# A four-layer transformer kernel on one core: layer 0 with x^T stored by tile, its last projections inside the block FFN, its indices outside the pool, and loads issued in the order of use

## The chip, the core and the metric

The kernel runs on one core of a Trainium2 chip. The core has a matrix engine (TensorE, here PE, with its weight loads as PEld), three other compute engines (VectorE is DVE, ScalarE is ACT, GpSimd is POOL), and an engine that mostly issues DMAs (SyncE, SP), which move data between HBM and the on-chip memory. The metric is the time of one launch on the device in microseconds (us), lower is better; a verdict compares medians of several runs.

## The reference, cut to what matters

Two batches of 1024 tokens with 1024 features pass through four layers, in fp32. Every layer is post-norm: `x = layernorm(x + attn(x))`, then `x = layernorm(x + ffn(x))`. The change touches layer 0 and the entry of layer 1. Batch 0 goes through all four layers before batch 1 begins.

```python
# layer 0, attention: 8 heads of 16 features
qk = (x @ Wqk_w.T + Wqk_b).reshape(b, n, 8, 16, 2)
v = (x @ Wv_w.T + Wv_b).reshape(b, n, 8, 16)
scores = einsum('bhqd,bhkd->bhqk', q, k)
attn = softmax(scores) / 128 ** 0.5
out = einsum('bhsl,bhlv->bhsv', attn, v) -> (b, n, 128)
x = layernorm(x + out @ Wo_w.T + Wo_b)
# layer 0, FFN: the features permuted, in 16 blocks of 64 -> 256 -> 64
t = x[:, perm].reshape(b * n, 16, 64)
t = gelu(einsum('bhd,hdm->bhm', t, up))
t = einsum('bhm,hmd->bhd', t, down).reshape(b * n, 1024)[:, unperm]
x = layernorm(x + t)
# layer 1, attention, its first step: a convolution of width 3 along the tokens, to 3 x 256 features
q, k, v = split(conv(x, conv_w) + conv_b, 3)
```

Layers 2 (a state space scan) and 3 (attention and a mixture with low-rank experts) are left as they are.

## The kernel before, in words

**Where things lie.** `x` holds one batch on chip, tokens on the 128 partitions, in 8 token tiles of 1024 features. `xT` is its transpose, features on partitions, in 8 tiles `k` of 128 features by 1024 tokens, with a column of margin at each end. Weights come into a pool `w` of 8 buffers of 512 KB, in turn. `ps` are the 8 banks of the matmul accumulator (PSUM), also taken in turn. Small vectors live in pools that open and close with the layer's stages; a tile that takes the place of another one in such a pool waits for its last reader.

**Order.** In layer 0 and at the entry of layer 1 the order of the work is written out by hand (`manual_schedule`): each engine issues its instructions in program order, and SP issues the DMAs in program order too, so that a DMA that waits for something holds up all DMAs behind it on SP. Gathers and scatters by index are issued by POOL.

**Layer 0, `l0(b)`.** First all eight tiles of `x` are loaded for batch 0 (`load_x`, before `l0` is called; for batch 1 the tiles are loaded by the end of the last layer, as they come free), and tiles 0 to 3 are turned into `xT` (`to_xT`, L130). Then `l0` issues its loads in this order: the three parts of `wqkv`, `wo`, the row of the bias `l0_bo`, two `up` and two `down`, and in its own pool `bqkv` and `idx`, the permutation. A *half* `th` is 512 tokens, four token tiles.

1. `qkv(s, th, scalar)` (L257) makes q, k or v for a half; for q and k, eight small DMAs spread the heads over the partitions.
2. `maxima(th)` computes the scores once for the maximum of each row (L292), with the remaining `qkv` steps between.
3. `attend(th, extra)` computes for each of 16 steps `n` (two groups of four heads, eight tiles of keys) the scores again (L327), their exponentials (ACT, L335) and the outputs (PE, L345); `done(g)` (copy `oT` L352, transposes L355) normalizes a group into `ao`. `extra[n]` is other work, placed behind step `n`'s outputs. In `attend(1)` it is the projection of the first half.
4. `project(tt)` transposes one tile of `ao` (L388), copies it on DVE to `aoT` (L390), multiplies it by `wo` in two matmuls of 512 columns (L393), adds them to `x` (`add_x`, L152) and takes the norm's statistics. `line(th, first, n)` spreads over the steps of the stage that runs beside: `first` of four tiles, then the roots and the scaling of all four, then four times `to_xT`. The list `n` gives the step of each.
5. `store(th)` writes a half of `xT` to HBM as `xd`, in eight DMAs of 256 KB, one for each feature tile, with runs of 2 KB (L399). `gather(th, n)` reads it back, by `idx`, with one indirect DMA for each tile `t` of 128 permuted features (L406).
6. `blocks(th, extra)` is the block FFN of a half. For each `j` of 8: `ups(j)` (four matmuls, L424), `gelus(j)` on ACT (L432), `downs(j)` (four matmuls, L442), a copy `o` (DVE, L454) and an indirect scatter into `yd` (POOL, L455). `ups(j+1)` stands ahead of `downs(j)`; `extra[j]` comes behind `downs(j)`.
7. `back(th)` loads `yd` (L473), and `add_y(tt, ys)` transposes it and adds it to `x`. For half 0 this runs beside `blocks(1)`, for half 1 at the entry of layer 1.

Between `attend(1)` and `blocks(0)` nothing runs beside: `done(1)`, `project(4)` and `project(5)` stand by themselves; `project(6)`, `project(7)`, roots, scaling and `to_xT` of the second half lie in `blocks(0)` at j = 0, 0, 1, 2, 2, 3, 3; `store(1)` is at j = 3, `gather(1)` at 5, 6 and 7.

**Entry of layer 1, `l1_attn(b)`.** Four small loads (`l1_convb` first, L85) go to a pool that takes the place of layer 0's. The convolution of a half is computed in a form with four products of half the length: `conv(th, co)` for each of six output tiles `co`. Its `load()` fetches the weights g0, g1, g2 (`w<-l_conv`, L80); for batch 0 and the first half, DVE computes t = g0 + g2 + g1 and t - 2 g1 from them (L599, L600, L601) and SP stores both to `cvd` (L603); everywhere else they are loaded from there. `sums0(j)` computes on DVE, in two pieces of four feature tiles each, a sum or difference of neighbouring tokens (L579) into a quarter of `qh` or `kh`, which `call(j, k)`, the convolution's matmuls (L612), read. `cb2` (L563) is twice the bias. The order is: c0's load and arithmetic, `sums0(0)`, `sums0(1)`, c1's load and arithmetic, the loads of `yd` half 1 (L652), then the matmuls, the rest of the sums, and the `add_y` of tiles 4 to 7 between them.

Of the kernel before, what the change touches and what calls it, by code (L numbers as in the profile page):

```python
# [17 lines left out]
P = 128  # L18
# [3 lines left out]
NT = S // P  # L22
# [5 lines left out]
class Net:  # L28
# [7 lines left out]
    def __init__(self, ctx, tc, ins, out):  # L36
        self.tc, self.nc, self.i, self.out = tc, tc.nc, ins, out
        nc = self.nc
        self.const = ctx.enter_context(tc.tile_pool(name="const", bufs=1))
        self.wp = ctx.enter_context(tc.tile_pool(name="wp", bufs=WB))  # L40
        self.bp = ctx.enter_context(tc.tile_pool(name="bp", bufs=2))
        self.sp = ctx.enter_context(tc.tile_pool(name="sp", bufs=3))
        self.pp = ctx.enter_context(tc.tile_pool(name="pp", bufs=8, space=PSUM))
        self.dp = ctx.enter_context(tc.tile_pool(name="dp", bufs=1, space=DRAM))
        self.count = 0
        self.evacs = 0

# [12 lines left out]
        nc.gpsimd.memset(self.one, 1.0)  # L60

        self.sel = c.tile([P, 4, 32], F, name="sel")
        nc.sync.dma_start(self.sel, self.i["l2_sel"])


    def nm(self, s):
# [146 lines left out]

    def l0(self, b):
        nc, i = self.nc, self.i
        wqkv = [self.w(i["l0_wqkv"][j]) for j in range(3)]
        wo = self.w(i["l0_wo"])
        row = self.row("l0_bo")
        up = [self.w(i["l0_up"][j]) for j in range(2)]
        down = [self.w(i["l0_down"][j]) for j in range(2)]  # L220
        xd, yd = [[self.dp.tile([D, HALF], F, name=self.nm(n)) for _ in range(2)] for n in ("xd", "yd")]
        with self.tc.tile_pool(name=self.nm("l0a"), bufs=1) as lp, self.tc.tile_pool(name=self.nm("l0b"), bufs=2) as tp:
            bias = self.param(lp, "l0_bqkv", [P, 3])
            idx = self.param(lp, "l0_perm", [P, KD], I)

            def piece(name):
                return lp.tile([P, HALF], F, tag="t", bufs=24, name=self.nm(name))
# [86 lines left out]
                        nc.vector.tensor_tensor(qT[g][th], qT[g][th], p, ALU.add)  # L314
                    yield

            def attend(th, extra):
# [55 lines left out]
                for n in range(N):  # L373
                    if n + 1 < N:
                        exps(n + 1)
                    if n + 2 < N:
                        scores(n + 2)
                    outputs(n)
                    if n == NT:
                        done(0)  # L380
                    for f in extra.get(n, []):
                        f()
                done(1)


            def project(tt):
                p = self.ps()
                nc.tensor.transpose(p[:, :P], ao[:, tt, :], self.ident)  # L388
                aoT = tp.tile([P, P], F, tag="aoT", name=self.nm("aoT"))
                nc.vector.tensor_copy(aoT, p[:, :P])  # L390
                for nh in range(2):
                    p = self.ps()
                    nc.tensor.matmul(p, aoT, wo[:, nh * HALF : (nh + 1) * HALF], start=True, stop=True)  # L393
                    self.add_x(tt, nh, p)
                self.ln_stats(tt)

            def store(th):
                for k in range(KD):
                    nc.sync.dma_start(xd[th][k * P : (k + 1) * P, :], self.xcols(k, th * HALF, HALF))  # L399

            ts = {0: [], 1: []}

# [6 lines left out]
                    )  # L409
                    ts[th].append(t)  # L410

            def blocks(th, extra):

                gls = {}

# [42 lines left out]
                    )  # L458

                ups(0)  # L460
                gelus(0)
                for j in range(KD):
                    if j + 1 < KD:
                        ups(j + 1)
                        gelus(j + 1)
                    downs(j)
                    for f in extra.get(j, []):
                        f()
# [21 lines left out]
            def at(extra, n, f):  # L490
                extra.setdefault(n, []).append(f)

            got = {}
            with self.tc.manual_schedule():
# [17 lines left out]
                m = maxima(1)  # L512
                attend(0, {n: [lambda: next(m)] for n in range(16)})
                e = line(0, project, (0, 1, 3, 4, 5, 6, 7, 8, 9))
                at(e, 9, lambda: store(0))
                at(e, 9, lambda: gather(0))
                attend(1, e)
                project(4)
                project(5)
                e = line(1, project, (-1, -1, 0, 0, 1, 2, 2, 3, 3))  # L520
                del e[-1]
                at(e, 3, lambda: store(1))
                for n in (5, 6):
                    at(e, n, lambda: gather(1, 2))
                at(e, 7, lambda: gather(1, 4))
                blocks(0, e)
                ys = back(0)
                e = line(0, lambda tt: self.add_y(tt, ys), (2, 3, 3, 4, 5, 6, 6, 7, 7))
                blocks(1, e)
# [6 lines left out]
    def l1_attn(self, b, yd, op):  # L536
        nc, i = self.nc, self.i
        row = self.row("l1_projb")
        with self.tc.tile_pool(name=self.nm("l1a"), bufs=1) as lp, self.tc.tile_pool(name=self.nm("l1s"), bufs=2) as spool:
# [20 lines left out]
            kh = lp.tile([P, 8, HALF], F, name=self.nm("kh"))  # L560
            u0 = lp.tile([P, HALF], F, name=self.nm("u0"))
            cb2 = lp.tile([P, 6], F, name=self.nm("cb2"))
            nc.vector.tensor_scalar(cb2, cb, 2.0, None, ALU.mult)  # L563
            if b == 0:
                self.cvd = self.dp.tile([6, 2, P, D], F, name=self.nm("cvd"))

# [24 lines left out]
            def conv(th, co):  # L591
# [3 lines left out]
                def load():  # L595
                    g = [self.w(i["l1_conv"][co, 0])]
                    if b == 0 and th == 0:
                        g1, g2, t = self.w(i["l1_conv"][co, 1]), self.w(i["l1_conv"][co, 2]), self.w()
                        nc.vector.tensor_tensor(t, g[0], g2, ALU.add)  # L599
                        nc.vector.tensor_tensor(t, t, g1, ALU.add)  # L600
                        nc.vector.scalar_tensor_tensor(g1, g1, -2.0, t, ALU.mult, ALU.add)  # L601
                        for n, f in enumerate((t, g1)):
                            nc.sync.dma_start(self.cvd[co, n], f)  # L603
                        w["w"] = [t, g1, g[0], g2]
                    else:
                        es = [self.w(self.cvd[co, n]) for n in range(2)]
                        w["w"] = es + g + [self.w(i["l1_conv"][co, 2])]
# [26 lines left out]
                return load, [lambda j=j, k=k: call(j, k) for j in range(4) for k in range(KD)], last  # L634

            def sums0(j):
                for g in range(2):
                    ks = slice(4 * g, 4 * g + 4)
                    sums(nc.vector, 0, ks, [(j, (qh, kh)[j // 2][:, ks, 256 * (j % 2) : 256 * (j % 2) + 256])])


# [2 lines left out]
            c0, c1 = conv(0, 0), conv(0, 1)  # L644
            with self.tc.manual_schedule():
                c0[0]()
                sums0(0)
                sums0(1)
                c1[0]()
                ys = [t for q in range(4) for t in (vh[:, q, :HALF], vh[:, q, HALF:])]  # L650
                for k, t in enumerate(ys):
# [1359 lines left out]
```

## Time and profile before

| what | value |
|---|---|
| runs of the kernel | 5103.77, 5097.98, 5096.71 us; median 5097.98 |
| the profiled execution | 5091.48 us, span in the trace 5089.7 us |
| mean granted clock of PE | 0.966 |
| busy: PE, PEld, DVE, ACT, POOL | 91%, 44%, 62%, 38%, 41% |
| the queues of SP's DMAs | 683.88 MB, 46.6% of 16 engines |

The span is from the first instruction to the last; the execution's own time is 1.8 us longer. The runs lie within 0.14% of each other. Times below "at" some point are microseconds from the start of the span. Batch 0's layer 0 runs from the start to about 326 us, batch 1's from 2545 to about 2858.

### The profile page before, as it was taken

How to read it: one execution, taken by the hardware profiler on the slowest of the kernel's cores; microseconds unless marked ns; L12 is line 12 of the kernel's file. 1: busy time of each engine (PE TensorE's matmuls, PEld its weight loads, DVE VectorE, ACT ScalarE, POOL GpSimd, SP SyncE). 2: the span in 40 equal slices, each digit the busy share in tenths (PEclk: the TensorE clock that was granted, in tenths of full speed). 3: DMA queues.
4: the chain of work that ended last, by engine and by line, in shares of the span. 5: the costliest groups of instructions: out<-in, count | busy, mean ns of one | idle time of the engine just before them, and what ended most of it. 6: DMA issues, size and time to landing. Idle time of an engine off the chain costs nothing. (4 is left out here: it accounts for less than half of the span.)

```text
span 5089.7 us, 49066 instructions
## 1 busy us (share of the span) xinstructions
PE 4656.9 (91%) x16584; PEld 2227.5 (44%) x16584; DVE 3152.2 (62%) x4322; ACT 1941.6 (38%) x3973; POOL 2094.1 (41%) x1259
## 2 busy tenths in 40 slices
PE   8989989988888889999999899899888988899999
PEld 3347745433333333454433576554333333334544
DVE  5453256389999996215365422652999999953153
ACT  2431232377665662001024212324776756510010
POOL 2013121089888994100020320201887989831010
PEclk9999999999999999999999999999999999999999
DMA  2144312488878997201211532113888889961100
GB/s 89 36 160 144 98 49 75 135 220 232 236 207 239 254 253 221 73 33 46 73 44 40 180 116 85 55 52 117 217 224 227 218 240 249 248 210 60 55 20 33
DMA packets 254862, 707.98 MB, mean 139 GB/s; under 512 B 37008, under 2 KB 54544, under 8 KB 254612
## 3 DMA queue, kind: packets, MB, share of 16 engines
q1 hardware_dynamic: 248340, 683.88, 46.6%
q0 software_dynamic: 6272, 20.98, 1.2%
q8 instruction: 132, 2.16, 0.2%
q14 instruction: 118, 0.97, 0.1%
HBM read 599.60 MB, written 86.25 MB: 135 GB/s over the span
## 5 line engine op out<-in xcount | busy, mean ns | idle before, releaser
L1299 POOL TENSOR_TENSOR h<-h,br 128x1024 f32<-128x1024 f32 x512 | 1205.7, 2372 | 105.8 <-DMA h<-dxd 71.1
L1306 PE MATMUL ps<-hl,rep 128*128 128x512 f32 x1024 | 733.5, 720 | 176.2 <-DVE h L1313 143.5
L1308 ACT ACTIVATE ps<-ps,l_Alog 128x512 f32<-128x512 f32 x1024 | 662.5, 662 | 554.4 <-PE ps L1306 551.8
L1313 DVE TENSOR_TENSOR_SCAN h<-ps,hst,h 128x512 f32<-128x512 f32 x512 | 633.4, 1282 | 19.9 <-ACT ps L1308 13.4
L1324 DVE TENSOR_TENSOR h<-h,ps 128x1024 f32<-128x1024 f32 x512 | 616.8, 1205 | 2.1 <-ACT hst L1321 2.0
L1313 DVE TENSOR_TENSOR_SCAN h<-ps,h 128x512 f32<-128x512 f32 x512 | 599.3, 1211 | 16.2 <-ACT ps L1308 16.1
L1421 PE MATMUL ps<-xT,w 128*128 128x512 f32 x1024 | 546.0, 620 | 10.1 <-DVE h L1313 8.9
L1306 PEld LDWEIGHTS ps<-hl,rep 128*128 128x128 f32 x1024 | 200.5, 197 | 600.3 <-DVE h L1313 436.0
L1626 POOL TENSOR_TENSOR x<-x,row 128x1024 f32<-128x1024 f32 x48 | 112.3, 2351 | 795.7 <-PE ps L130 795.7
L152 DVE TENSOR_TENSOR x<-x,ps 128x512 f32<-128x512 f32 x192 | 129.1, 684 | 435.1 <-PE ps L1803 143.9
L104 PE MATMUL ps<-xT,w 128*128 128x512 f32 x768 | 335.9, 592 | 0.0
L1335 PE MATMUL ps<-h,sel 128*32 128x512 f32 x2048 | 297.1, 630 | 5.6 <-DVE h L1324 5.6
L1459 PE MATMUL ps<-w,w 128*128 128x512 f32 x512 | 279.2, 629 | 21.3 <-DMA w<-yd 14.3
L177 ACT ACTIVATE rs<-mv 128x1 f32<-128x1 f32 (+2 forms) x88 | 17.9, 203 | 705.4 <-DVE mv L171 705.0
L1421 PEld LDWEIGHTS ps<-xT,w 128*128 128x128 f32 x1024 | 190.7, 195 | 204.4 <-issue 165.8
L104 PE MATMUL ps<-w,xT 128*128 128x512 f32 (+1 forms) x768 | 278.3, 522 | 0.0
L1366 PE MATMUL ps<-xT,w 128*128 128x512 f32 x512 | 271.6, 630 | 6.2 <-DVE h L1313 6.2
L1124 DVE SCALAR_TENSOR_TENSOR ps<-xp,l_convw,ps 128x512 f32<-128x512 f32 x192 | 145.1, 756 | 200.8 <-ACT ps L1119 196.2
L767 POOL TENSOR_TENSOR s<-s,l1r 128x512 f32<-128x512 f32 x64 | 66.5, 1040 | 487.8 <-DVE l1r L766 481.9
L1800 PE MATMUL ps<-w,xT 128*128 128x512 f32 x512 | 225.7, 594 | 0.0
L1244 POOL TENSOR_TENSOR e<-e,one 128x512 f32<-128x512 f32 x64 | 81.5, 1274 | 349.5 <-ACT xp L1116 220.3
L104 PEld LDWEIGHTS ps<-xT,w 128*128 128x128 f32 x768 | 145.0, 189 | 183.0 <-issue 178.1
(289 smaller groups left out, 7452.1 us busy)
## 6 DMA issues: line engine op xcount, KB each, us to landing
h<-dxd SPq DMA_DIRECT2D x512, 512.0 KB, 7.9
w<-l_in SPq DMA_DIRECT2D x128, 512.0 KB, 6.4
w<-l_out SPq DMA_DIRECT2D x96, 512.0 KB, 6.9
w<-l_conv SPq DMA_DIRECT2D x54, 512.0 KB, 3.8
w<-cvd SPq DMA_DIRECT2D x36, 512.0 KB, 3.3
w<-l_fw SPq DMA_DIRECT2D x32, 512.0 KB, 4.5
xcd<-xo SPq DMA_DIRECT2D x64, 256.0 KB, 3.9
xi<-xcd SPq DMA_DIRECT2D x64, 256.0 KB, 8.7
```

Of the source, the lines that this page charges most:

```text
L104: self.nc.tensor.matmul(out, lhsT, rhs, start=j == 0, stop=j == n - 1)
L1124: nc.vector.scalar_tensor_tensor(p, xp[:, k : k + HALF], cw[:, c, k : k + 1], p, ALU.mult, ALU.add)
L1299: nc.gpsimd.tensor_tensor(hs[k], hs[k], norms[of(k)[0]][1].unsqueeze(1).to_broadcast([P, 2, HALF]), ALU.mult)
L1306: nc.tensor.matmul(dA[k, m], rep[:, 4 * m + q, :], hl[u, c][:, jj, :], start=True, stop=True)
L1308: nc.scalar.activation(dA[k, m], dA[k, m], AF.Exp, scale=A[:, g : g + 1])
L1313: nc.vector.tensor_tensor_scan(hs[k][:, m, :], dA.pop((k, m)), hs[k][:, m, :], hst[:, g : g + 1] if u else 0.0, ALU.mult, ALU.add)
L1324: nc.vector.tensor_tensor(hs[k], hs[k], norms[of(k)[0]][3].unsqueeze(1).to_broadcast([P, 2, HALF]), ALU.mult)
L1335: nc.tensor.matmul(py[u, c][32 * j : 32 * j + 32, :], self.sel[:, q, :], hs[k - 1 + j // 2][:, j % 2, :], start=False, stop=q == 3,)
L1366: nc.tensor.matmul(p, w["w"][:, k * P : (k + 1) * P], self.xcols(k, u0, HALF), start=k == 0, stop=k == KD - 1)
L1421: nc.tensor.matmul(p, w["w"][:, k * P : (k + 1) * P], self.xcols(k, u * HALF, HALF), start=k == 0, stop=k == KD - 1)
L1459: nc.tensor.matmul(p, y[:, cc, t * P : (t + 1) * P], wt[:, cc * HALF : (cc + 1) * HALF], start=c2 == 0 and cc == 0, stop=last,)
L1800: nc.tensor.matmul(p, self.xcols(k, tt * P, P), wt[k][:, ns], start=k == 0, stop=False)
```

## The change

- *Loads.* Only tiles 0 to 3 of `x` are loaded before `l0`. In `l0`, part 1 and then part 0 of `wqkv` are loaded first, for batch 0 then `bqkv`, `idx`, `sel` (a constant of layer 2 that was the first load of the program) and tiles 4 to 7 of `x`, and then part 2 of `wqkv`, `wo` and the rest.
- *Indices outside the pool.* `bqkv` and `idx` are constants, loaded once, and no longer tiles of layer 0's pool in each batch.
- *Stores by tile.* `store(tt)` writes one token tile of `xT`, all features, in one DMA of 512 KB with 1024 runs of 512 bytes. The four of half 0 stand at n = 6 to 9 of `attend(1)`, each behind the `to_xT` of its tile; the four of half 1 at j = 3, 3, 4, 4 of `blocks(0)`.
- *Projections.* `turn_o` (the transpose and the copy `aoT`) is split from `project`. In `attend(1)` it stands ahead of the outputs of the same step, the rest behind them. The last `done(1)` runs inside `blocks(0)`, behind `ups(0)`; projections 4 to 7 lie at j = 0, 0, 1, 1 of `blocks(0)`, with their transposes ahead of `downs(j)`; roots and scaling at j = 2, `to_xT` at 3, 3, 4, 4.
- *Layer 1.* For batch 0, `sums0(0)` stands between L600 and L601 of `conv(0, 0)`; in both batches it comes in three pieces (feature tiles 0 and 1, 2 and 3, 4 to 7). `cb2` comes behind `sums0(1)`.

In the changed kernel's lines: `turn_o` is L401 and L403, the projection's matmuls L410, `store` L415, the gather L425, ups, gelus, downs, `o` and the scatter L443, L451, L461, L473, L474, `back` L496, the sums L601, the weight arithmetic L621, L622 and L625, the stores to `cvd` L627, the convolution's matmuls L636, `cb2` L674.

```diff
@@ __init__
-        nc.sync.dma_start(self.sel, self.i["l2_sel"])
+        self.idx = c.tile([P, KD], I, name="idx")
+        self.bqkv = c.tile([P, 3], F, name="bqkv")
@@ l0
-        wqkv = [self.w(i["l0_wqkv"][j]) for j in range(3)]
+        wqkv = {j: self.w(i["l0_wqkv"][j]) for j in (1, 0)}
+        if b == 0:
+            for t, name in ((self.bqkv, "l0_bqkv"), (self.idx, "l0_perm"), (self.sel, "l2_sel")):
+                nc.sync.dma_start(t, i[name])
+            for tt in range(4, NT):
+                self.load_x(0, tt)
+        wqkv[2] = self.w(i["l0_wqkv"][2])
...
-            bias = self.param(lp, "l0_bqkv", [P, 3])
-            idx = self.param(lp, "l0_perm", [P, KD], I)
+            bias = self.bqkv
+            idx = self.idx
@@ attend(th, extra, ahead={})
                     if n + 2 < N:
                         scores(n + 2)
+                    for f in ahead.get(n, []):
+                        f()
                     outputs(n)
...
-                done(1)
+                if th == 0:
+                    done(1)
+                return done
@@ project, store
+            aoT = {}
+
+            def turn_o(tt):
                 p = self.ps()
                 nc.tensor.transpose(p[:, :P], ao[:, tt, :], self.ident)
-                aoT = tp.tile([P, P], F, tag="aoT", name=self.nm("aoT"))
-                nc.vector.tensor_copy(aoT, p[:, :P])
+                aoT[tt] = tp.tile([P, P], F, tag="aoT", name=self.nm("aoT"))
+                nc.vector.tensor_copy(aoT[tt], p[:, :P])
+
+            def project(tt):
+                if tt not in aoT:
+                    turn_o(tt)
...
-            def store(th):
-                for k in range(KD):
-                    nc.sync.dma_start(xd[th][k * P : (k + 1) * P, :], self.xcols(k, th * HALF, HALF))
+            def store(tt):
+                nc.sync.dma_start(
+                    xd[tt // 4].rearrange("(k p) t -> p k t", p=P)[:, :, tt % 4 * P : (tt % 4 + 1) * P],
+                    self.xT[:, :, 1 + tt * P : 1 + (tt + 1) * P],
+                )
@@ blocks(th, extra, ahead={}, first=None)
                 ups(0)
+                if first:
+                    first()
                 gelus(0)
                 for j in range(KD):
                     if j + 1 < KD:
                         ups(j + 1)
                         gelus(j + 1)
+                    for f in ahead.get(j, []):
+                        f()
                     downs(j)
@@ the order of layer 0
-                at(e, 9, lambda: store(0))
+                for n in range(4):
+                    at(e, 6 + n, lambda n=n: store(n))
                 at(e, 9, lambda: gather(0))
-                attend(1, e)
-                project(4)
-                project(5)
-                e = line(1, project, (-1, -1, 0, 0, 1, 2, 2, 3, 3))
-                del e[-1]
-                at(e, 3, lambda: store(1))
+                done = attend(1, e, {n: [lambda tt=tt: turn_o(tt)] for tt, n in enumerate((0, 1, 3, 4))})
+                e = line(1, project, (0, 0, 1, 1, 2, 3, 3, 4, 4))
+                for n, tt in ((3, 4), (3, 5), (4, 6), (4, 7)):
+                    at(e, n, lambda tt=tt: store(tt))
...
-                blocks(0, e)
+                ahead = {n: [lambda t=t: turn_o(t), lambda t=t: turn_o(t + 1)] for n, t in ((0, 4), (1, 6))}
+                blocks(0, e, ahead, lambda: done(1))
@@ l1_attn
-            nc.vector.tensor_scalar(cb2, cb, 2.0, None, ALU.mult)
...
                         nc.vector.tensor_tensor(t, t, g1, ALU.add)
+                        if co == 0:
+                            sums0(0)
                         nc.vector.scalar_tensor_tensor(g1, g1, -2.0, t, ALU.mult, ALU.add)
...
             def sums0(j):
-                for g in range(2):
-                    ks = slice(4 * g, 4 * g + 4)
+                for k0, k1 in ((0, 4), (4, KD)) if j else ((0, 2), (2, 4), (4, KD)):
+                    ks = slice(k0, k1)
...
                 c0[0]()
-                sums0(0)
+                if b:
+                    sums0(0)
                 sums0(1)
+                nc.vector.tensor_scalar(cb2, cb, 2.0, None, ALU.mult)
                 c1[0]()
@@ net_kernel
-        for tt in range(NT):
+        for tt in range(4):
             net.load_x(0, tt)
```

More of the change, by code (lines that the diff above doesn't have):

```diff
@@ L315, in maxima, with attend @@
                     yield
-            def attend(th, extra):
+            def attend(th, extra, ahead={}):
                 steps = [(g, kt) for g in range(2) for kt in range(NT)]
@@ L382, in attend @@
                         f()
-                done(1)
-            def project(tt):
+                if th == 0:
[3 more added lines that the diff above has]
+            def turn_o(tt):
                 p = self.ps()
                 nc.tensor.transpose(p[:, :P], ao[:, tt, :], self.ident)
-                aoT = tp.tile([P, P], F, tag="aoT", name=self.nm("aoT"))
-                nc.vector.tensor_copy(aoT, p[:, :P])
+                aoT[tt] = tp.tile([P, P], F, tag="aoT", name=self.nm("aoT"))
[3 more added lines that the diff above has]
+                    turn_o(tt)
                 for nh in range(2):
                     p = self.ps()
-                    nc.tensor.matmul(p, aoT, wo[:, nh * HALF : (nh + 1) * HALF], start=True, stop=True)
+                    nc.tensor.matmul(p, aoT[tt], wo[:, nh * HALF : (nh + 1) * HALF], start=True, stop=True)
                     self.add_x(tt, nh, p)
                 self.ln_stats(tt)
-            def store(th):
-                for k in range(KD):
-                    nc.sync.dma_start(xd[th][k * P : (k + 1) * P, :], self.xcols(k, th * HALF, HALF))
+            def store(tt):
[3 more added lines that the diff above has]
+                )
             ts = {0: [], 1: []}
@@ L410, in gather, with blocks @@
                     ts[th].append(t)
-            def blocks(th, extra):
+            def blocks(th, extra, ahead={}, first=None):
                 gls = {}
```

## The prediction

> **What bounds the kernel now.** I read the page first (busy shares by engine and by slice), then the timeline of TensorE (PE) through the two stretches that the change touches, then the waits of PE there, then the timelines of the DMA issuer (SP) and of VectorE (DVE) at the entry of layer 1. From the page:
>
> ```profile
> span 5089.7 us, 49066 instructions
> PE 4656.9 (91%) x16584; PEld 2227.5 (44%) x16584; DVE 3152.2 (62%) x4322; ACT 1941.6 (38%) x3973; POOL 2094.1 (41%) x1259
> ```
>
> PE is busy 91% of the span, so a change that leaves its work alone can only win its idle time and the time it runs on a halved clock. The change touches layer 0 (0 to 326 us for batch 0, 2545 to 2858 for batch 1) and the first 30 us of layer 1 after each. PE's timeline at the start of both batches (start, length, what, and in brackets the idle time before it and who ended it):
>
> ```profile
> 4.82 6.34 PE L130 MATMUL ps<-ident,x 128*128 128x128 f32 x32 [4.82 <-DMA x<-x]
> 17.44 15.40 PE L257 MATMUL ps<-xT,w 128*128 128x512 f32 x32 [6.28 <-DMA w<-l_wqkv]
> ...
> 2550.33 13.98 PE L257 MATMUL ps<-xT,w 128*128 128x512 f32 x32 [1.11 <-ACT xT L99]
> ```
>
> Batch 0 loses 6.28 us because w[1] of wqkv stands tenth on SP's queue, behind eight tiles of x; batch 1, whose loads are early, loses 1.11. The second stretch lies between attend(1) and blocks(0), batch 0:
>
> ```profile
> 230.22 0.66 PE L355 MATMUL ps<-ident,oT 128*128 128x128 f32 x4 [0.79 <-DVE oT L352]
> 232.01 0.47 PE L388 MATMUL ps<-ident,ao 128*128 128x128 f32 x1 [1.14 <-DVE ao L364]
> 232.87 3.78 PE L393 MATMUL ps<-w,aoT 128*128 128x512 f32 x4 [0.38 <-DVE aoT L390]
> 236.45 0.42 PE L388 MATMUL ps<-ident,ao 128*128 128x128 f32 x1
> 239.03 3.53 PE L393 MATMUL ps<-w,aoT 128*128 128x512 f32 x4 [2.16 <-DVE aoT L390]
> 242.49 3.70 PE L424 MATMUL ps<-t,w 64*128 64x512 f32 x16
> ...
> 253.61 1.96 PE L393 MATMUL ps<-w,aoT 128*128 128x512 f32 x4 [2.36 <-DVE aoT L390]
> ...
> 284.68 3.70 PE L424 MATMUL ps<-t,w 64*128 64x512 f32 x16 [0.90 <-DMA t<-xd,l_perm]
> ```
>
> The last attention output ends at 229.43, and blocks(1) begins at 284.68: 55.25 us. PE goes back and forth with DVE, and two projections run at half speed (3.78 and 3.53 us for what takes 1.96 later). The third stretch is the entry of layer 1, SP and PE:
>
> ```profile
> 296.02 24.87 SPq L80 DMA_DIRECT2D w<-l_conv  x3
> 329.44 0.33 SPq L85 DMA_DIRECT2D l_convb<-l_convb  x1
> ...
> 335.31 10.04 PE L612 MATMUL ps<-qh,w 128*128 128x256 f32 x32 [9.08 <-issue]
> 346.90 3.72 PE L612 MATMUL ps<-kh,w 128*128 128x256 f32 x16 [1.56 <-DVE kh L579]
> ```
>
> The conv weights are fetched during blocks(1), l1_convb only after the last scatter (it takes the place of the indices), and PE idles 9.08 us.
>
> **Part 1, loads in the order of use.** A 512 KB load takes about 1.3 us of the queues (4.84 MB in 12 us, 404 GB/s). With four tiles of x and then w[1], w[0] the fifth and sixth transfers land near 10 and 11 us, before the transposes (and their copies) end at about 11.8. L257 then starts at 11.8 instead of 17.44, with the clock still up (granted 1.00 from 8.2 to 11.2 us, 0.50 from 17.4 to 20.0 after the wait), and takes 13.98 instead of 15.40 as in batch 1, so it ends at 25.8 against 32.68 (last end 32.8): 6.9 less. x 4 to 7 are transfers 10 to 13, landed by 18, and needed at 25.8. bqkv lands with the first ones, where it came at 26.83. The rest of the start up to L292 has no wait but PE's own, so all 6.9 passes on; batch 1 gains nothing. Ends: 5.3 (clock cold) and 8.0.
>
> **Part 2, the transposes of ao ahead of outputs in attend(1).** Four times PE waits for the copy aoT, 0.48, 0.38, 0.47 and 0.38 us (179 to 197 us); outputs (1.07) now covers each. 1.7 per batch at most; DVE is still in the norm statistics at the second and fourth, so I take 1.3, ends 0.5 and 1.7.
>
> **Part 3, projections 4 to 7 inside blocks(0).** With time zero at the end of the last output and the rows' lengths, PE's new order reads: ups(0) 2.0; L355 0.66; ups(1) to 4.5; two transposes to 5.0 (ao is ready at 3.75: 1.74 after L355 begins); downs(0) 1.94 to 6.9 (its gelus: table load 1.28, then 2.06, ready at 4.4); projections 4 and 5, 3.9, to 10.8; ups(2), transposes 6 and 7, downs(1) and projections 6 and 7 to 19.0; ups(3), downs(2), ups(4), downs(3) to 26.7. DVE, with 2.8 us of adds and statistics for each projection, ends tile 7 at 21.8, the roots give scales from 25.2 to 28.1, so transposes 4 and 5 (26.7) don't wait. Then two transposed pairs and the remaining blocks: downs(7) ends at 44.1. Against 55.25 that is 11.1 less (11.8 in batch 1, 55.95). Scatter yd(7) must await the landing of yd(6) (scatters stand 4.4 apart), which makes y about 1.0 later for add_y: 10.1 and 10.8.
>
> **Part 4, stores by tile.** They must keep up with this. The first four are issued at the transposes (204.7 to 218.1); the gather came at 227.63 and now may come near 223, so t is there for ups(0) at zero. The other four are issued at 29.6, 30.3, 34.2 and 35.3; the first gather of blocks(1) follows scatter yd(5) at 40.65, and needs 3.4 to land: 44.05, just in time. Each store has 1024 runs of 512 bytes, 64 on each of 16 queues, in place of 2 KB runs. Packets of 2 KB take 86 ns and of 4 KB 162 (16 queues times the window, over their number), which extends to 29 ns for 512 bytes: 1.9 us a store. The one transfer of 512-byte runs in the trace is sel's:
>
> ```profile
> DMA packets 159, 0.13 MB, mean 71 GB/s; under 512 B 16, under 2 KB 144, under 8 KB 159
> q1 hardware_dynamic: 159, 0.13, 36.6%
> ```
>
> From 0.8 to 2.6 us the queues were busy 10.5 us; less 15 packets of 4 KB and 16 small ones that leaves some 57 ns for each of the 128: 3.7 us a store. I take 2.6, nearer the row of the same kernel's stores. Four in a row, 1.9 in all for fixed latency and 3.5 for gather: blocks(1) then begins at 35+4x2.6=45.4, 1.3 late in each batch (ends 0 and 5.7).
>
> The Trainium skill ("DMA: Bandwidth & Descriptors", Specifications) gives 512 bytes as enough for line rate. By that page the 1.3 would be 0 and the sum 2.6 better; the row of sel disagrees, though it stands at the cold start.
>
> **Part 5, indices outside the pool, sums first.** l1_convb no longer waits for the last scatter, but in the new order it stands on SP ahead of the three conv loads, and it still waits for the last matmul of downs(7) of blocks(1), which reads the pool that is given back. That matmul ends at 324.33. So four small loads (1.75 us, as at 329.44), then the weights at 326.3: the third lands at 2.1+3x1.3 later, 331.8; in the old run DVE's L599 began at 326.44 with all three there. Behind it L600 to 334.3, the first sums to 334.9: PE starts at 335.1, as before. But L601 now follows the sums and ends at 337.9 instead of 333.96; the stores to cvd and the loads of the next conv come behind it on SP, L599 of that one at 345.6 (was 341.97), and the sums of kh behind it at 350.5: L612's second stretch starts 3.7 late. PE has then idled 5.5 us; after 9.08 us of idling 32 calls took 10.04 against 7.07 when warm, after 1.56 nothing was lost. I add 1.3: 5.0 lost in batch 0 (ends 2 and 7). In batch 1 nothing is computed from the weights: its second load lands at 2863.3 and PE began at 2863.37 before; 0, ends -1 and +2. cb2's wait (3.72 us at 331.37) is gone, but the later weights cover it.
>
> The granted clock after those 9.08 us was 0.50 from 335.3 to 338.7 and 0.63 from 338.7 to 342.0. The Trainium skill ("TensorE: Matmul & The Clock Gate", Part 1: The HAM clock gate) says that an idle window of about 3.4 us halves the clock, and that it takes a busy window as long to bring it back. As an estimate by that page, half of 3.4 would be lost after any such idling, 1.7 and not 1.3, and the sum would be 0.4 worse; the 10.04 against 7.07 of the row speaks for more still, 3.0 after the longer wait.
>
> Sel, bqkv and idx, once each, and 16 fewer SP issues a batch hide beside PE.
>
> **The sum**: -6.9 -2x1.3 -(10.1+10.8) +2x1.3 +5.0 = -22.8 us. The profiled execution took 5091.48 (span 5089.7), 6.5 below the median 5097.98: 5068.7 by its own time, 5075 as a median. About 0.2%, 10 us, is what a measurement can tell from no change.
>
> **The rivals.** (a) *Stores slow enough to lose.* Once a store takes over 4.4 us (the pace of the first four transposes) they queue in both halves, and the price is eightfold. With store time d, blocks(0) begins at 4d-18.9, blocks(1) 35+4d after it. At d=5.2 all gains are gone; from 5.7 (89 ns a packet) the kernel is slower by 10; at d=7 by 30: 5128. For it: the large SP transfers in the trace have 128 runs each. Against: sel's 57 ns. 8%.
> (b) *Conv weights cost more, stores 3.7:* 5.7 a batch in Part 4 and 7+2 in layer 1 leave -10 (5088), no telling. 8%.
> (c) *Only half of Part 3* (PE waits for gelus or DVE): 5.3 of 10.5 a batch, so -12: 5086. 12%.
> (d) *The loads change nothing*, were the ring shared evenly by the transfers in flight: -16, 5082. 10%. For it: x's landing rises to 9.9 us.
> (e) *Stores that hide wholly*, at 1.9 us or less each: -25.4, 5072. For it: the rows of 2 and 4 KB. Against: sel's. 20%.
> The forecast itself, with its 1.3 a batch: 42%.
>
> **How the numbers follow.** 5075 is the likeliest. From 5064 (stores hidden, Part 5 at 2, load gain 8, Part 2 at 1.7 give 5068; 4 more since the runs stand between 5.2 and 12.3 above the profiled execution) to 5088, which takes in (c), (d) and the edge of (b). Faster 0.84 (forecast, c, d, e), same 0.08 (b), slower 0.08 (a).
>
> **What would show it.** L257 starting near 12 us with no wait for w; no wait of the projections for aoT; 229.43 to the first matmul of blocks(1), 55.25, becoming 44 to 47, its wait naming t's gather if stores are late; l1_convb ahead of the conv loads right after downs(7), DVE waiting for w<-l_conv near the entry of layer 1, and L612's second stretch late. The forecast is wrong if a store's landing exceeds 7 us, or the entry of layer 1 comes out shorter.

## The result and the profile after

The changed kernel takes 5082.59 us in the median of 7 runs (5077.50 to 5090.05), the kernel before 5097.98 in 7 runs beside it (5091.97 to 5103.77): a ratio of 0.9971 with a 95% interval of 0.9960 to 0.9982, some 15 us faster. The forecast was 5075, with a range of 5064 to 5088. Its profiled execution took 5081.22. The page, span and busy time:

```profile
span 5079.5 us, 49085 instructions
...
PE 4651.2 (92%) x16584; PEld 2223.0 (44%) x16584; DVE 3150.1 (62%) x4324; ACT 1941.1 (38%) x3973; POOL 2094.6 (41%) x1259
```

PE has 5.7 us less of busy time (4656.9 before), and the rest of the 10.2 us by which the span fell is idle time. To see where, I cut both batches at the same five points: the first matmul of q, k and v; the end of the last attention output; the first matmul of blocks(1); the last transposes of layer 0; and the first matmul of the third convolution (c2), behind the last transposes in layer 1's entry. All lengths in us, batch 0 / batch 1, from PE's timelines:

| kernel | qkv starts (batch 0) | to the last output | to blocks(1) | to the last transposes | to c2 | batch 1, qkv to c2 |
|---|---|---|---|---|---|---|
| before | 17.44 | 211.99 / 208.11 | 55.25 / 55.95 | 39.58 / 42.16 | 57.70 / 49.91 | 356.13 |
| before, profiled again | 17.19 | 212.37 / 208.32 | 54.86 / 57.51 | 40.01 / 41.71 | 58.99 / 49.87 | 357.41 |
| changed | 11.26 | 207.08 / 205.84 | 48.11 / 48.71 | 42.78 / 41.58 | 66.45 / 52.35 | 348.48 |

Batch 0 is 6.3 us ahead at c2 (375.68 against 381.96) and batch 1 gains 7.7 more, 14 in all (16.7 against the second profile of the kernel before). Between these two stretches, where nothing was edited, the profiled executions of this study took 2168 to 2180 us, so single totals say little about a few us, and the stages say more.

**The start** went as forecast. PE's timeline of the changed kernel (start, length; in brackets the idle time before and who ended it):

```profile
11.26 14.01 PE L264 MATMUL ps<-xT,w 128*128 128x512 f32 x32 [0.35 <-DVE xT L98]
```

L264 (L257 of before) no longer waits for weights, only 0.35 us for a copy.

**From the last output to blocks(1)** 7 us were won in each batch, not 10. PE, then DVE, ACT and POOL in the same stretch:

```profile
215.09 3.25 PE L352 MATMUL ps<-pt,v 128*32 128x512 f32 x24
218.27 1.99 PE L443 MATMUL ps<-t,w 64*128 64x512 f32 x8
223.53 0.66 PE L362 MATMUL ps<-ident,oT 128*128 128x128 f32 x4 [3.27 <-DVE oT L359]
...
229.85 3.70 PE L410 MATMUL ps<-w,aoT 128*128 128x512 f32 x8
...
266.45 3.70 PE L443 MATMUL ps<-t,w 64*128 64x512 f32 x16 [0.68 <-DMA t<-xd,idx]
```

```profile
222.78 0.69 DVE L359 COPY oT<-ps 128x512 f32<-128x512 f32 x1 [15.82 <-remote]
```

```profile
222.86 1.28 ACT L451 ACT_TABLE_LOAD   x1 [5.62 <-remote]
```

```profile
211.38 1.14 POOL L425 DMA_INDIRECT t<-xd,idx  x1 [171.48 <-DMA xd<-xT]
...
220.34 0.95 POOL L425 DMA_INDIRECT t<-xd,idx  x1 [0.30 <-issue]
```

The projections (L410) run without a wait for aoT, and blocks(1) waits 0.68 us for its gather. But the copy oT, which needs only the last output, begins at 222.78, 4.4 us after that output ended at 218.34, and PE waits 3.27 for it. "remote" means that the trace names no releaser. In batch 1 the same wait is 3.33. ACT is late too: its first step for the gelus, which needs ups(0), begins at 222.86, though ups(0) ended at 220.26. For most of that time POOL issues the eight gathers, 211.38 to 221.29. In the kernel before, the copy began 0.04 us after the last output:

```profile
229.47 0.69 DVE L352 COPY oT<-ps 128x512 f32<-128x512 f32 x1 [11.42 <-PE ps L345]
```

The next stage, blocks(1) up to the last transposes, takes 3.2 us longer in batch 0 and 0.6 less in batch 1. In batch 0 PE's granted clock was 0.50 from 283 to 287 us, after PE had waited for `y`, and one ups(j) took 3.78 us there instead of 1.99.

**The entry of layer 1, batch 0**, lost more than forecast. SP, DVE and PE:

```profile
309.36 0.33 SPq L86 DMA_DIRECT2D l_convb<-l_convb  x1
...
311.31 1.38 SPq L81 DMA_DIRECT2D w<-l_conv  x3
```

```profile
318.73 1.22 DVE L621 TENSOR_TENSOR w<-w,w 128x1024 f32<-128x1024 f32 x1 [7.24 <-DMA w<-l_conv]
...
332.76 1.23 DVE L621 TENSOR_TENSOR w<-w,w 128x1024 f32<-128x1024 f32 x1 [5.73 <-DMA w<-l_conv]
```

```profile
321.96 9.79 PE L636 MATMUL ps<-qh,w 128*128 128x256 f32 x32 [10.77 <-DVE qh L601]
337.70 5.32 PE L636 MATMUL ps<-kh,w 128*128 128x256 f32 x16 [5.95 <-DVE kh L601]
```

l1_convb stands at the front, right behind the last matmul of downs(7) (ends at 309.30). The three weight loads behind it release DVE 7.4 us after they are issued; the next three are issued at 325.14 and release it 7.6 later. The first matmul comes 12.73 after the last transposes instead of 11.05, and the second stretch waits 5.95 instead of 1.56.

### The profile page after: what moved, and what is told of

It reads as the page before. It is cut to its first block, busy times and chain, and to the rows that moved or that the text cites. A ratio compares the mean times of both kernels' runs of the same rounds, so it can differ in the third digit from the quotient of the medians.

```text
span 5079.5 us, 49085 instructions
## 1 busy us (share of the span) xinstructions
PE 4651.2 (92%) x16584; PEld 2223.0 (44%) x16584; DVE 3150.1 (62%) x4324; ACT 1941.1 (38%) x3973; POOL 2094.6 (41%) x1259
## 4 chain that ended last, share of the span: by engine, by line
PE 59%; DVE 16%; DMA 9%; POOL 6%; issue 5%; ACT 3%; SPq 1%; another core or an unknown queue 1%; POOLq 0%; DVEq 0%; ACTq 0%
PE ps L105 21%; DVE h L1339 8%; PE ps L636 6%; PE ps L1666 4%; PE ps L1826 4%; POOL h L1325 4%; PE ps L1447 3%; DMA h<-dxd 2%; DMA xi<-xcd 2%; PE ps L131 2%; PE ps L334 2%; PE ps L264 2%; PE ps L1361 2%; PE ps L1332 2%; DVE h L1350 2%
```

## The experiments

All ratios are to the kernel before, run beside them on the same chip (median 5092.36 for the first four, 5095.25 for the next four); the changed kernel was not run again beside them. Theories: Q, that SP's order costs the entry; G or P, that POOL's gathers hold back what PE reports to other engines; S, that the many packets of the 512-byte stores do that; I, that the new place of the indices does; D, that gathers do where they stand closely and PE, ACT and DVE are all at work; T, that the bytes in flight do.

**1. Small loads of layer 1 behind the convolution's first loads.**

```diff
-            cb = self.param(lp, "l1_convb", [P, 6])
...
+            cb, bq, bk, bo = [lp.tile([P, n], F, name=self.nm(a)) for a, n in (("cb", 6), ("bq", 8), ("bk", 8), ("bo", 2))]
...
                 c0[0]()
+                for t, a in ((cb, "l1_convb"), (bq, "l1_bq"), (bk, "l1_bk"), (bo, "l1_bo")):
+                    nc.sync.dma_start(t, i[a])
```

> The changed kernel, with the four small loads of layer 1 (l1_convb, bq, bk, bo) issued behind the three weight loads of the first convolution and its stores, not ahead of them. Theory (SP's order costs the entry): the weights land during blocks(1); the first weight arithmetic starts within 1 us of the last xT copy instead of 7.2 later, the first convolution matmul some 5 to 7 us after the last transpose instead of 12.7, and its second stretch waits under 3 us instead of 5.95. Batch 0 gains 6 to 9 us against the changed kernel, batch 1 about 1: total near 5073. Rival (the sums put between the weight arithmetic cost the entry): the second stretch still waits over 4 us and the gain is at most 3: near 5080.

5072.46 us, ratio 0.9960 (0.9947 to 0.9973). PE in the entry of batch 0:

```profile
313.62 3.69 PE L633 MATMUL ps<-qh,w 128*128 128x256 f32 x16 [3.43 <-DVE qh L598]
...
330.74 6.31 PE L633 MATMUL ps<-kh,w 128*128 128x256 f32 x16 [9.49 <-DVE kh L598]
```

The first matmul comes 5.4 us after the last transposes, as Q said, but the second stretch waits longer, 9.49, since its sums stand on DVE behind the next weights, and those behind the stores on SP. To c2 it is 61.55 us (batch 0) and 45.26 (batch 1), 4.9 and 7.1 less than in the changed kernel (in batch 1, 1 was expected). Q holds for the first wait; for the second, the rival's sign came (over 4 us), though not its size (a gain of at most 3).

**2. Stores by feature, as before**, and **3. stores of two token tiles** (runs of 1 KB).

```diff
-            def store(tt):
-                nc.sync.dma_start(
-                    xd[tt // 4].rearrange("(k p) t -> p k t", p=P)[:, :, tt % 4 * P : (tt % 4 + 1) * P],
...
+            def store(th):
+                for k in range(KD):
+                    nc.sync.dma_start(xd[th][k * P : (k + 1) * P, :], self.xcols(k, th * HALF, HALF))
```

```diff
-                    xd[tt // 4].rearrange("(k p) t -> p k t", p=P)[:, :, tt % 4 * P : (tt % 4 + 1) * P],
-                    self.xT[:, :, 1 + tt * P : 1 + (tt + 1) * P],
+                    xd[tt // 4].rearrange("(k p) t -> p k t", p=P)[:, :, tt % 4 * P : (tt % 4 + 2) * P],
+                    self.xT[:, :, 1 + tt * P : 1 + (tt + 2) * P],
```

> The changed kernel with the stores as before: eight DMAs of 256 KB with runs of 2 KB for each half, at n = 9 of attend(1) and j = 4 of blocks(0). In the changed kernel DVE's copy oT starts 4.4 us after the last attention output, in both batches, and ACT's gelus in blocks(1) come one by one, 2 us apart. Theory S (the many packets of 512-byte stores hold back PE's signals some 10 us later): oT starts within 0.1 us of the last output and the gelus come in fours; the gather comes 4 to 5 us later, which takes back some 2 us; from the last output to blocks(1) 44 to 47 us instead of 48.1; total 3 to 8 below the changed kernel, 5075 to 5080. Theory G (gathers in flight beside a busy PE hold back its signals): the delay moves with the gathers into the first blocks, and the stretch stays at 48 or grows by 2; total 5083 to 5088.

> The changed kernel with stores for two token tiles at a time: four DMAs of 1 MB with runs of 1 KB instead of eight of 512 KB with 512 bytes, so half the packets, issued with the later tile of each pair. Theory S (packets): oT starts 0 to 2 us after the last output instead of 4.4; total 3 to 9 below the changed kernel. Theory G (gathers): 4.4 us as before, total unchanged within 2 us.

Ratios 0.9973 (0.9963 to 0.9983) and 0.9983 (0.9974 to 0.9992): neither beats the changed kernel's 0.9971. In the second the gathers begin at 216.60, and oT starts on time, at 218.47; now the next step of the same chain is late, and later gelus of blocks(1) come singly (ACT, one of them):

```profile
218.47 0.69 DVE L359 COPY oT<-ps 128x512 f32<-128x512 f32 x1 [11.42 <-PE ps L352]
222.81 0.26 DVE L365 RECIPROCAL l0rv<-ps 128x16 f32<-128x16 f32 x1 [3.65 <-PE ps L441]
```

```profile
276.18 0.60 ACT L449 ACTIVATE g<-ps 128x512 f32<-128x512 f32 x1 [1.42 <-PE ps L459]
```

The delay moved with the gathers, and with 2 KB runs it is still there, as G said; S falls. From the last output to blocks(1) it is 47.31 / 47.79 us, and 46.56 / 48.16 in the third, where oT starts 3.3 us late and PE waits 2.1 for it: neither the 0 to 2 of S nor the 4.4 of G. Stores by tile cost nothing and bring little as long as the gathers hold back PE's results.

**4. The first half's gathers spread.**

```diff
-                at(e, 9, lambda: gather(0))
+                at(e, 9, lambda: gather(0, 2))
...
+                e[0].insert(0, lambda: gather(0, 2))
+                e[1].insert(0, lambda: gather(0, 2))
...
+                def first():
+                    done(1)
+                    gather(0, 2)
...
-                blocks(0, e, ahead, lambda: done(1))
+                blocks(0, e, ahead, first)
```

> The changed kernel with only two gathers of the first half at n = 9 of attend(1); two more come behind done(1), two behind downs(0) and two behind downs(1) of blocks(0). Theory G (gathers in flight beside PE's last outputs hold back its signals): oT starts within 1 us of the last output instead of 4.4, and the stretch to blocks(1) falls from 48.1 to 44 to 46; total 4 to 8 below the changed kernel. Theory S (packets of the stores): oT stays over 3 us late, total within 2 us of the changed kernel.

5076.01 us, ratio 0.9965 (0.9952 to 0.9978).

```profile
218.87 1.99 PE L443 MATMUL ps<-t,w 64*128 64x512 f32 x8
220.79 0.65 PE L362 MATMUL ps<-ident,oT 128*128 128x128 f32 x4
...
262.08 3.70 PE L443 MATMUL ps<-t,w 64*128 64x512 f32 x16 [0.63 <-DMA t<-xd,idx]
```

L362 has no wait; in both batches oT starts 0.04 us after the last output. The stretch is 43.14 / 43.89 us, against 48.11 / 48.71 in the changed kernel and 44.1 in Part 3 of the prediction. S and the order of the program (oT waiting for something that was moved) are out: the same order on PE, DVE and ACT, the same stores, no delay. The total gained less than the 4 to 8 us expected: the two ratios are 3 us apart, within their intervals.

**5. Before, with constant indices alone**, and **6. the first experiment with the indices back in the pool.**

```diff
+        self.idx = c.tile([P, KD], I, name="idx")
+        nc.sync.dma_start(self.idx, self.i["l0_perm"])
...
-            idx = self.param(lp, "l0_perm", [P, KD], I)
+            idx = self.idx
```

```diff
-        self.idx = c.tile([P, KD], I, name="idx")
...
-            for t, name in ((self.bqkv, "l0_bqkv"), (self.idx, "l0_perm"), (self.sel, "l2_sel")):
+            for t, name in ((self.bqkv, "l0_bqkv"), (self.sel, "l2_sel")):
...
-            idx = self.idx
+            idx = self.param(lp, "l0_perm", [P, KD], I)
```

> The kernel before with one thing of the change: the indices are a constant, loaded once, and no longer a tile of layer 0's pool. In the kernel before, PE's results reach ACT and DVE without delay while the second half's eight gathers run (gelus in fours of 2.06 us from 291.4 us on); in the changed kernel and in all four variants so far they come late there. Theory I (the place of the indices makes gathers hold back PE's signals): the gelus of blocks(1) come singly, about 2 us apart, during the gathers; the stretch from the first matmul of blocks(1) to the last transpose grows from 39.6 by 2 to 4 us, and l1_convb no longer waits for the last scatter: total 0 to 8 slower than before. Theory D (density: gathers back to back while PE, ACT and DVE are all at work): no late gelus; total within 4 of before.

> The kernel of the first experiment (small loads of layer 1 behind the convolution's first loads), with the indices back in layer 0's pool, loaded in each batch. Theory I: oT starts within 0.2 us of the last output in both batches, from there to blocks(1) 43 to 45 us instead of 48 to 49, gelus of blocks(1) in fours; 8 to 14 faster than the first experiment. Theory D: oT 4.4 us late as in the first experiment, total within 3 of it.

The fifth is slower than before: 1.0025 (1.0016 to 1.0034), 13 us by the ratio and 11 by the medians. A gelu comes singly in its blocks(1) (297.43), as theory I says, but the stage does not grow (39.31 against 39.58). The sixth is 0.9965 (0.9953 to 0.9978), no better than the first experiment's 0.9960, with oT as late as there; so theory I falls. What the indices' place does is seen at the entry of layer 1 (fifth, SP and PE):

```profile
325.97 0.33 SPq L87 DMA_DIRECT2D l_convb<-l_convb  x1
...
327.90 1.38 SPq L82 DMA_DIRECT2D w<-l_conv  x3
```

```profile
340.30 9.89 PE L614 MATMUL ps<-qh,w 128*128 128x256 f32 x32 [12.50 <-DVE qh L581]
```

l1_convb has gone from behind the conv loads to the front, as in the changed kernel, and the entry takes 63.61 us instead of 57.70 or 58.99: this one edit costs 4.6 to 5.9 us at the entry of batch 0 and 1.2 in batch 1. The total grew by more; of the 11 to 13 the stages that I cut show only some 2 to 5 (c2 of batch 0 comes 6.0 to 7.5 later, batch 1 takes 2.8 to 4.1 less), and the rest stays open.

**7. Experiments 1 and 4 together** (their two diffs), and **8. with three more edits** (the diff against the seventh; `c0[3]` and `c1[3]` are the two convolutions' `fetch`).

```diff
+                def fetch():
+                    w["g"] = [self.w(i["l1_conv"][co, n]) for n in range(3)] + [self.w()]
...
+                if b == 0:
+                    c0[3]()
+                    c1[3]()
                 c0[0]()
...
+                sums0(2)
                 c1[0]()
...
                 calls(c0, 0)
-                sums0(2)
...
-                at(e, 7, lambda: gather(1, 4))
...
+                for n in range(4):
+                    e.setdefault(n, []).insert(0, lambda: gather(1, 1))
                 blocks(1, e)
```

> The first and the fourth experiment together: small loads of layer 1 behind the convolution's first loads, and the first half's gathers spread. If the two gains are independent (5 at the entry of layer 1; 5 before blocks(1) in each batch), the sum is 12 to 16 below the changed kernel, a ratio to the kernel before of 0.9940 to 0.9950. Rival: what is won ahead of blocks(1) is lost to later gathers or y, and the ratio stays at 0.996.

> The seventh, with three more edits: the second half's last four gathers come one by one inside blocks(1) (behind downs(0) to downs(3)) and not together at j = 7; for batch 0 the weights of the second convolution are fetched ahead of the first one's stores on SP; and the sums of kh stand ahead of the second convolution's weight arithmetic on DVE. In the first experiment PE waited 9.49 us for those sums. Theory (orders on SP and DVE): that wait falls below 4 us, gelus of blocks(1) come in fours, blocks(1) takes 1 to 3 less in each batch: 7 to 13 faster than the seventh, ratio near 0.993. Rival (the weights' landing, or the buffers they need, set the entry): the wait moves to the second convolution's first matmul and at most 3 are won.

The seventh: 5067.05 us, 0.9944 (0.9930 to 0.9958), as expected, and the rival's 0.996 is out; it is more than the ratios of 1 and 4 add up to (0.9954), which their intervals allow. The eighth: 5053.65 us, 0.9914 (0.9899 to 0.9929), 42 to 44 us below the kernel before and the fastest of the study. PE in its entry of batch 0:

```profile
307.71 9.84 PE L646 MATMUL ps<-qh,w 128*128 128x256 f32 x32 [3.43 <-DVE qh L606]
317.38 3.62 PE L646 MATMUL ps<-kh,w 128*128 128x256 f32 x16
```

The wait for the sums of kh (9.49 in the first experiment, 6.54 in the seventh) is gone, and the entry takes 55.14 us instead of 59.83 in the seventh. Gathers one by one in blocks(1) gave 2.0 us in batch 0 (39.86 against 41.84) and nothing in batch 1 (40.01 against 39.98), but ACT's gelus now come in fours in both (269.17 and 272.95, 2.06 and 2.07 us), where the seventh had single ones (270.35 and 273.11): a second place where spreading the gathers removes the delay. From the seventh to the eighth the total fell by 13 us in the medians, at the upper end of what was expected; the stages account for 6.5 of it (c2 of batch 0), and the rest stays open.

**9. The kernel before, profiled once more**, and **10. plain loads in place of the first half's gathers.**

```diff
                     t = piece("t")
+                    if th == 0:
+                        nc.sync.dma_start(t, xd[0][j * P : (j + 1) * P, :])
+                        ts[th].append(t)
+                        continue
```

> The kernel before, unchanged, profiled once more. Its profile shows PE's results reaching ACT at once while the second half's gathers run in blocks(1) (gelus in fours of 2.06 us), where the kernel before with constant indices showed them late. If the delay belongs to the order of the program, this profile shows fours again and the stretch from blocks(1) to the last transpose at 39.6 and 42.2 us; if it comes and goes from one execution to the next, this one shows single gelus too, and no part of the change made it.

> The changed kernel with the first half's eight gathers replaced by eight plain loads of 256 KB that SP issues from the same buffer: the same bytes in the same place of the order, with the permutation of the first half left out. Theory P (POOL's making of the gathers' descriptors holds back PE's signals): oT starts within 0.2 us of the last output in both batches, the stretch to blocks(1) is 43 to 44 us instead of 48.1 and 48.7. Theory T (the traffic into the chip's memory beside a busy PE does it): oT is 2 to 5 us late as before, or later, since the loads come closer together.

The ninth took 5095.33 us beside 5097.69. ACT in blocks(1), first as first profiled, then as profiled again:

```profile
291.40 2.06 ACT L432 ACTIVATE g<-ps 128x512 f32<-128x512 f32 x4 [1.48 <-PE ps L424]
295.19 2.06 ACT L432 ACTIVATE g<-ps 128x512 f32<-128x512 f32 x4 [1.72 <-PE ps L424]
```

```profile
293.28 0.60 ACT L432 ACTIVATE g<-ps 128x512 f32<-128x512 f32 x1 [3.61 <-PE ps L442]
296.01 3.79 ACT L432 ACTIVATE g<-ps 128x512 f32<-128x512 f32 x7 [2.14 <-PE ps L424]
```

So the late reports exist in the kernel before too, and no part of the change made them. What spared the execution first profiled stays open. They cost the kernel before little (40.01 us against 39.58 in blocks(1)), since nothing on PE's path then waited for a report.

The tenth took 5067.87 us beside 5097.69 (one run each). oT starts at 218.10, 0.04 after the last output; the stretch is 43.16 / 44.03 us.

```profile
218.10 0.69 DVE L359 COPY oT<-ps 128x512 f32<-128x512 f32 x1 [11.42 <-PE ps L352]
```

Busy time of PE, PEld, DVE, ACT and POOL over two us of the last outputs, then PE's granted clock, the DMA share and GB/s, first with plain loads, then in the changed kernel with gathers:

```profile
216.00:218.00 2.00, 2.00 (x18) 0.42 (x10) 0.00 (x0) 0.96 (x2) 0.00 (x0) 1.00 0.93 343
```

```profile
217.00:219.00 2.00, 2.00 (x14) 0.63 (x8) 0.00 (x0) 0.24 (x1) 1.48 (x2) 1.00 0.82 211
```

The same bytes, and more of them per second (343 GB/s against 211), leave PE's reports on time; in the same kernel's second half, which is still gathered, gelus come singly again (271.41 us). T falls: not the traffic, but the gathers that POOL issues hold the reports back. Whether it is POOL's work of making them or the queue that they run in is not told apart by these runs.

## Why the prediction was right, and which of its terms were not

The total (5075, measured 5082.59) lies in the range and the kernel is faster, as forecast, with two thirds of the gain. Term by term:

- *Part 1, -6.9.* L264 starts at 11.26 (11.8 forecast) and ends 7.6 us earlier. The wait for kT at the first scores fell as well (2.85 to 1.76), but the rows behind it ran slower, and at 89 us the lead was still 7.5. By the second half of attention it was 9.8, and these 2.3 are luck of the execution. After a wait of 2.8 us in both kernels the clock granted to PE came back sooner in the changed one (1.00 from 92.5 to 95.4 us and on to 105; before 0.68 from 100.0 to 103.5 and 0.52 from 109 to 111), so that 24 score matmuls took 5.35 us for 6.00 and, a few us on, eight outputs and eight scores 1.06 and 1.14 for 1.86 and 1.99. Experiment 1, with the same order there, has 6.00, 1.86 and 1.99 again.
- *Part 2, -1.3 a batch.* From the second half of attention to the last output the lead grows from 9.8 to 11.1, 1.3 us. In batch 1 qkv to the last output is 2.3 shorter.
- *Part 3, -10.1 and -10.8.* The order of PE's work was worked out rightly: without the delay the stretch takes 43.1 to 44.0 (experiments 4 and 10), 44.1 was forecast. The step that failed is the assumption that a result is seen by the next engine when the matmul ends. In the kernel before, the gathers ran while PE went back and forth with DVE; the change moved them under the last outputs and put ups(0) behind these, so that the late reports fell on PE's path: 4.7 to 5.0 us in each batch (48.11 and 48.71, outside the 44 to 47 given as a sign, against the two experiments). For a later `y` I had 1.0 in blocks(1); it came to 3.2 in batch 0, with the halved clock at 283 us, and to -0.6 in batch 1.
- *Part 4, +1.3 a batch.* It is 0, and rival (e) was right on this term: the first gather of the second half (263.07, and 2797.74 in batch 1) waits for no store. One store in the trace of the changed kernel, GB/s in 40 slices of 0.125 us:

```profile
GB/s 0 0 0 0 0 0 0 0 0 49 274 291 295 283 303 274 299 283 295 295 283 299 279 279 115 0 0 0 0 0 131 0 0 0 0 0 0 0 0 0
DMA packets 1041, 0.54 MB, mean 108 GB/s; under 512 B 16, under 2 KB 1040, under 8 KB 1040
```

  1024 packets in 1.8 us, 28 ns each on 16 queues: the extension of the rows of 2 and 4 KB (29 ns), not the row of sel (57). The rate is 290 GB/s, against 404 for the 4 KB loads at the start and some 380 for the stores of 2 KB runs in the kernel before (222.0 to 224.4 us). The Trainium skill ("DMA: Bandwidth & Descriptors", Specifications) gives 512 bytes as enough for line rate; the forecast made from it, no cost, came true, though the rate here is below that of the larger packets.
- *Part 5, +5.0 and 0.* In batch 0 the mechanism was right, the size was not: 8.75 (66.45 against 57.70), beyond the end of 7. Three weight loads took 7.4 and 7.6 us from issue to use, where I had 5.5 (the sum written there, 2.1+3x1.3, is 6.0), so that the first matmul was late too. Then the clock: the second stretch took 5.32 us for 16 calls, 1.70 more than the 3.62 of the next one, after 5.95 of idling (granted clock 0.50 from 337.7 to 340.0); I had put 1.3. The prediction's estimate from the Trainium skill ("TensorE: Matmul & The Clock Gate", Part 1: The HAM clock gate), 1.7, agrees with this row. It is no fixed price: the same row lost 1.5 us in experiment 10 after 6.10 of idling and 3.0 in experiment 4 after 6.43. In batch 1, where I had 0, it cost 2.4, beyond the end of 2: the small loads stand at the front there too, the loads of `cvd` are issued behind them, 2.6 us after the last transposes and no longer ahead of these, and PE waits 6.17 us for them, where it had waited 4.85 for the sums.

Together: parts 1 and 2 brought 3.9 more than forecast (2.3 of it luck with the clock), parts 3 and 4 to the last transposes 6.5 less, and part 5 cost 6.2 more. That is, but for rounding, the 8.9 between -22.8 and the 13.9 of the stages. The total was thus nearer than its terms, of which two missed by over 6 us. Two slips of the working changed nothing: the stores by tile save 8 SP issues a batch and not 16, and the 4 us added below 5068 come to 1.3 by the runs named there (6.5 less 5.2). Of the rivals, (b) came nearest on layer 1 and (c) on the size of Part 3, for a reason that neither had.

## What to carry to other kernels

Taking a tile out of a pool removes one wait and may move a DMA: here four small loads went to the front of an in-order queue and cost more than the wait they were freed from, and issuing them behind the large loads made the two entries 12 us shorter (some 6 us by the ratios). When dependent work is moved next to indirect DMAs, ask who waits for PE's results during the gathers, and spread the gathers. And profile the kernel before twice: the execution that I forecast from had no late reports in blocks(1), the next one had.

## What the runs showed of the hardware that was not expected

While POOL issues indirect gathers back to back (eight in 9.9 us), PE's results can reach DVE and ACT late: 4.4 us for oT in batch 0 of the changed kernel, single gelus some 2 us apart in blocks(1), though PE's own records run on at full pace. Four gathers in a row, issued by 216.91 and moving data until 219 (experiment 4), did no harm to oT at 218.98, gathers one by one left the gelus in fours (experiment 8), and the same bytes loaded by SP did no harm at a higher rate. Nor is a row of gathers enough by itself: beside the eight of the kernel before (227.63 to 237.54), where PE idled between its matmuls, DVE's steps at 229.47, 232.53 and 236.69 began within 0.05 us of the matmul that they waited for. What else it takes is open. The profile computes the ends of matmuls and does not observe them, so it can't tell a late report from a matmul that ended late. Whether this also happens in executions that are not recorded can't be seen here; the runs' ratios go the same way, though within their intervals (0.9965 with the gathers spread against 0.9971, 0.9944 against 0.9960 on top of the first experiment).
